# A fused Mamba, attention and expert layer: the first batch's start, reordered

## The chip, the cores and the metric

The kernel runs on one core of a Trainium2 chip. The metric is the device time of one execution in microseconds, lower is better; the number given for a kernel is the median of its runs. The engines are named as the profile names them: PE multiplies matrices, DVE is VectorE, ACT is ScalarE, POOL is GpSimd, and SP issues all transfers of this kernel.

## The reference

One decoder layer over x of 32 batches, 256 tokens, 256 channels, in three blocks, each followed by a layer norm of x plus the block:

```
# 1. state space block, per batch
xc, res = split(x @ W_in.T + b_in)              # 512 channels each
u = silu(causal_conv3(xc) + conv_b)
dlt, Bm, Cm = split(u @ W_x.T)                  # 64, 16, 16
delta = softplus(dlt @ W_dt.T + b_dt)           # the step sizes
carry[t] = exp(delta * A) * carry[t-1] + delta * u * Bm   # 512 x 16 states,
y[t] = sum_n carry[t, :, n] * Cm[t, n]          # restarted every 64 tokens
x = layernorm(x + (y * silu(res)) @ W_out.T + b_out)
# 2. cross attention to ctx (256 tokens), 16 heads of 16
x = layernorm(x + attention(x, ctx))
# 3. experts: token block e of 32 goes through expert e of 8 (256 -> 704 -> 256)
x = layernorm(x + (silu(x @ w1[e]) * (x @ w3[e])) @ w2[e])
```

## The kernel before

All 32 batches go through one pipeline. A batch passes these stages, each a Python generator (a chain) that yields before its next piece of work:

- `pre(b)`: x is transposed on PE (L334) and copied to xT by ACT (L368). PE multiplies it by w_in (`ps_in`, L343). ACT scales the three taps of the convolution into `u` and `shifted` (L390), POOL adds them (L403), ACT evicts `sres` (L349) and applies Silu to `u` (L417) and `sres` (L420) between two table loads (L417, L359).
- `sizes(b)`: the step sizes. PE computes `ps_x` from u and w_x (L434), ACT evicts it as `xp` (L439), PE computes `ps_dt` from xp and w_dt, whose 65th row is b_dt (L343). Softplus is Abs and Relu of ps_dt on ACT (L462, L463), Exp of the first (L466), then on POOL for each of four column blocks a correction `lost` of three operations (L471 to L473), Ln on ACT (L475), and two POOL operations over all four blocks: `delta` (L477) and delta times u, written to `u` (L484). SP stores delta and u to `dd` in DRAM, each when it is ready, and loads C broadcast over partitions (`c_bc`).
- `scan()`: 16 steps a batch. Each loads a strip of dd broadcast over partitions (`ld`, two transfers), ACT computes `da`, the exponentials (`decays`, L561), VectorE the product `bu` (L583, with `b_bc` from PE, L531) and the recurrence `h` (L601). POOL multiplies h by c_bc (`weighted`, L616). After every four steps PE sums over the states into `y` (L630, `sums`), and VectorE multiplies it by sres (L646).
- `mixes`, `keys`, `queries`, `maxima`, `attns`, `finishes`: the projection `ps_out` and the first layer norm, then attention. `maxima` finds the row maxima of the scores (`tops`, L798). The first piece of `mixes` multiplies b_v, spread by VectorE (`bv`, L707), with w_o (`ps_bv`, L711).
- `units`: 32 expert units (L1057, L1119, L1137, L1148), each of one expert over two groups of four batches or of two experts over one group, whose weights come from `fetches` (w13 in transfers of 352 KB, w2 in three). A unit can begin when its batches are stored after attention. Where the first set of buffers is concerned, fetches begin at 50 us of the planner's clock.

The order on every engine is fixed when the kernel is built. `in_order` keeps a clock for each engine from estimated costs (`MM`, `EV`, `VE`, `GP`, and `ISSUE` for a transfer), asks each chain when its next piece can start, and takes the earliest, with a chain's `lag` as the tie breaker; a wait that a chain can't yet answer is `None`. So a chain that starts at another time shifts the order of all that comes later.

Each engine executes its queue in order, SP too: a transfer stands behind those issued before it. Ahead of all chains, the kernel issues the loads of x of batch 0 and of all weights by `dma`. Eight semaphores are used in turn for SP's transfers, so the issue of a transfer waits for the landing of the eighth before it.

Of the kernel before, what the change touches and what calls it, by code (L numbers as in the profile page):

```python
# [10 lines left out]
ALU = mybir.AluOpType  # L11
# [4 lines left out]
P = 128  # L16
B, L, D = 32, 256, 256
DI, NS, DTR = 512, 16, 64
NDC = DI // P
# [78 lines left out]
def decoder_kernel(ctx: ExitStack, tc: tile.TileContext, a: dict, out: bass.AP):  # L98
    nc = tc.nc
    clock = Clock()  # L100
    spend = clock.spend

    def dma(dst, src):

        nc.sync.dma_start(dst, src)  # L105
        spend("SP", ISSUE)
# [82 lines left out]

    w_dt = wp.tile([DTR + 1, DI], F32, name="w_dt")  # L190
    dma(w_dt[:DTR], a["w_dt"])
    for c in range(NDC):
        src = a["b_dt"][:, c : c + 1].rearrange("p o -> o p")
        dma(w_dt[DTR:, c * P : (c + 1) * P], src)
    one = wp.tile([P, 1], F32, name="one")
    nc.gpsimd.memset(one, 0.0)
    nc.gpsimd.memset(one[DTR : DTR + 1], 1.0)
# [4 lines left out]
    for j in range(NJ):  # L202
        for g in range(GB):
            at = a_all[:, j, g].rearrange("p k n -> p (k n)")
            dma(at, src[j, g].unsqueeze(1).to_broadcast([DL, NL, NDC * NS]))
    nc.scalar.preload_act_table_set("natural_log_exp_and_others")
    load_ctx(0)
    w_k, b_k = heads("k")
    w_v = weight("w_v", D, D)
# [4 lines left out]
    b_o = row("b_o")  # L214
    b_v = wp.tile([P, 2, 1], F32, name="b_v")
    dma(b_v, a["b_v"].rearrange("(k p o) -> p k o", p=P, o=1))

# [81 lines left out]

    MM = 0.47
    EV = {1: 0.47, 2: 0.6, 4: 1.06}
    VE = {1: 0.41, 2: 0.69}
    GP = {1: 0.7, 2: 1.27, 4: 2.36}

    def layernorm(tiles, t):
# [49 lines left out]
    def exps():  # L357

        nc.scalar.preload_act_table_set("natural_log_exp_and_others")  # L359
        spend("ACT", 1.28)  # L360

    def pre(b):

# [63 lines left out]
    def sizes(b):  # L427

        yield lambda: us[b][1] if b in us else None, "PE"
        u, t = us[b]  # L430
        yield from take(1, 3, t)
        ps = bank("ps_x")[:, :L]
        for k in range(NDC):
            nc.tensor.matmul(  # L434
                ps[:XP], w_x[:, k, :], u[:, k, :], start=(k == 0), stop=(k == NDC - 1)
            )
        yield spend("PE", NDC * MM), "ACT"
        xp = unit2.tile([P, L], F32, tag="xp", name=f"xp_{b}")
        nc.scalar.activation(xp[:XP], ps[:XP], AF.Identity, bias=one[:XP])  # L439
        t = spend("ACT", EV[1])  # L440
        done(1, t)
        xps[b] = xp
        bcds[b] = bcd.tile([NS, L], F32, tag="bcd", name=f"bcd_{b}")
        yield t, "SP"
        dma(bcds[b], xp[XP - NS : XP])
        yield from take(2, 3, t)
        pss = []
        for c2 in range(2):
            pss.append(
                product(  # L450
                    "ps_dt",
                    lambda j: [w_dt[:, (2 * c2 + j) * P : (2 * c2 + j + 1) * P]],
                    lambda j: [xp[: DTR + 1]],
                )
            )

        yield pss[0][1], "ACT"
        z = unit1.tile([P, NDC, L], F32, tag="delta", name=f"delta_{b}")
        e = unit1.tile([P, NDC, L], F32, tag="e", name=f"ez_{b}")
        for c2, (ps, t) in enumerate(pss):  # L460
            cc = slice(2 * c2, 2 * c2 + 2)
            nc.scalar.activation(e[:, cc], ps, AF.Abs)  # L462
            nc.scalar.activation(z[:, cc], ps, AF.Relu)  # L463
            t = spend("ACT", 2 * EV[2], t)
            done(1, t)
        nc.scalar.activation(e, e, AF.Exp, scale=-1.0)  # L466
        yield spend("ACT", EV[4]), "POOL"
        for c in range(NDC):

            lost = unit1.tile([P, L], F32, tag="lost", name=f"lost_{b}")  # L470
            nc.gpsimd.tensor_scalar(lost, e[:, c], 1.0, -1.0, op0=ALU.add, op1=ALU.add)  # L471
            nc.gpsimd.tensor_tensor(lost, e[:, c], lost, ALU.subtract)  # L472
            nc.gpsimd.tensor_tensor(z[:, c], z[:, c], lost, ALU.add)  # L473
            yield spend("POOL", 3 * GP[1]), "POOL" if c < NDC - 1 else "ACT"
        nc.scalar.activation(e, e, AF.Ln, bias=1.0)  # L475
        yield spend("ACT", EV[4]), "POOL"
        nc.gpsimd.tensor_tensor(z, z, e, ALU.add)  # L477
        yield spend("POOL", GP[4]), "POOL"
        while b >= 2 and b - 2 not in gated:
            yield lambda: gated.get(b - 2), "SP"  # L480
        dds[b] = bcd.tile([2, DI, L], F32, tag="dd", name=f"dd_{b}")
        dma(dds[b][0].rearrange("(c p) t -> p c t", p=P), z)
        load_c(b)
        nc.gpsimd.tensor_tensor(u, z, u, ALU.mult)  # L484
        t = spend("POOL", GP[4])
        yield t, "SP"
        dma(dds[b][1].rearrange("(c p) t -> p c t", p=P), u)
        spread[b] = t + 3.0
        del us[b]
# [4 lines left out]

    def pres():
        for b in range(B):
            yield lambda: 0.0 if len(us) < 2 else None, "PE"
            yield from pre(b)
        while silus:
            silus.pop(0)()  # L500
# [169 lines left out]

    def keys():

        for b in range(B):
            if b:
                load_ctx(b)
            t0 = clock.at["SP"] + LANDING
            ctxT = cts.pop(b)
            yield from take(1, 4, t0)
            ps, t = product(
                "ps_qk",  # L680
                lambda j: [w_k[:, k, j * P : (j + 1) * P] for k in range(2)],
                lambda j: [ctxT[:, k, :] for k in range(2)],
            )
            yield t, "ACT"
            flat = unit1.tile([P, 2, L], F32, tag="k_flat", name=f"k_flat_{b}")
            tk = biased(flat, AF.Identity, b_k, ps, 0)
            done(1, tk)
            yield tk, "SP"
            yield from spread_heads(b, kT, flat, kts)
            yield lambda: max(t0, attended[-1] if b else 0.0) if len(attended) >= b else None, "PE"  # L690
            yield from take(1, 2, t0)
            ps, t = product(
                "ps_v",
                lambda t: [ctxT[:, k, t * P : (t + 1) * P] for k in range(2)],
                lambda t: [w_v[:, k, :] for k in range(2)],
            )
            yield t, "ACT"
            nc.scalar.copy(v[:, :, :, :DK], ps.rearrange("p t (h d) -> p t h d", d=DK))
            vts[b] = spend("ACT", EV[2])
            done(1, vts[b])  # L700

    def mixes():


        yield lambda: spread.get(0), "DVE"
        bv = unit1.tile([P, 2, P], F32, tag="x1T", name="bv")
        nc.vector.tensor_copy(bv, b_v.to_broadcast([P, 2, P]))  # L707
        yield from take(1, 2, spend("DVE", 0.3))
        ps = bank("ps_bv")
        for k in range(2):  # L710
            nc.tensor.matmul(ps[:, :D], bv[:, k, :], w_o[:, k, :], start=(k == 0), stop=(k == 1))  # L711
        yield spend("PE", 2 * MM), "DVE"
        nc.vector.tensor_tensor(b_o, ps[:, :D], b_o, ALU.add)
        done(1, spend("DVE", VE[1]))
        for b in range(B):
            if b >= 2:
                yield lambda: stored[b - 2] + 3.0 if len(stored) >= b - 1 else None, "SP"
            load_x1(b)
            yield clock.at["SP"] + LANDING, "POOL"
            x1 = x1s[b]  # L720
            nc.gpsimd.tensor_tensor(
                x1, x1, b_out.unsqueeze(1).to_broadcast([P, 2, D]), ALU.add
            )
            spend("POOL", GP[2])
            yield lambda: gated.get(b), "PE"
            yield from take(1, 2, gated[b])
            yg = ygs.pop(b)
            ps, t = product(
                "ps_out",
                lambda t: [yg[:, k, t * P : (t + 1) * P] for k in range(NDC)],  # L730
                lambda t: [w_out[:, k, :] for k in range(NDC)],
            )
            yield t, "DVE"
            nc.vector.tensor_tensor(x1, ps, x1, ALU.add)
            t = spend("DVE", VE[2])
            done(1, t)
            t = yield from layernorm([x1[:, t, :] for t in range(2)], t)
            yield lambda: None if x1Ts else t, "PE"
            yield from take(1, 2, t)
            ps, t = transposes(x1)  # L740
            yield t, "ACT"
            x1T = unit1.tile([P, 2, L], F32, tag="x1T", name=f"x1T_{b}")
            nc.scalar.copy(x1T, ps)
            t = spend("ACT", EV[2])
            done(1, t)
            x1Ts[b] = x1T, t
            yield t, "POOL"
            nc.gpsimd.tensor_tensor(x1, x1, b_o.unsqueeze(1).to_broadcast([P, 2, D]), ALU.add)
            spend("POOL", GP[2])
# [406 lines left out]
    def units(bufs):  # L1156
# [9 lines left out]

    xs_at[0] = 10.0
    chains = [
        Chain(decays(), -3.0),
        Chain(weighted(), -2.0),  # L1170
        Chain(scan(), 0.0),
# [79 lines left out]
```

## Time and profile before

| | |
|---|---|
| median of 3 runs | 2941.95 us (2936.0 to 3024.58) |
| the profiled execution | 2947.31 us, its span 2945.6 us |
| PE busy | 2539.0 us (86%) |
| VectorE busy | 2386.1 us (81%) |
| ACT busy | 2041.6 us (69%) |
| POOL busy | 2035.6 us (69%) |
| TensorE clock granted, mean | 0.935 |
| first recurrence (h L601) starts | 71.55 us |
| last recurrence starts | 2631.8 us |

The span is from the first to the last instruction. A line of the timeline gives the start and the length of an instruction in us, its engine and line, what it writes and reads, and in brackets the idle time of its engine before it with what ended that. In a group of the page the two numbers ahead of the second bar are the busy time in us and the mean length in ns; behind it stands the idle time before the group. A matmul of the program in float32 appears as two in the trace (x8 for four).

### The profile page before, as it was taken

The page shows a single profiled execution, that of the slowest core. Times are in us where ns is not written, and L with a number is a line of the kernel's source. Part 1 is how long each engine was busy: PE and PEld are TensorE (multiplying, and loading weights), DVE is VectorE, ACT ScalarE, POOL GpSimd, SP SyncE. Part 2 cuts the span into 40 slices and gives each one's busy share as a digit, 9 for nine tenths or more (in the row PEclk, how much of TensorE's full clock was granted, in tenths as well). Part 3 has the DMA queues.
Part 4 walks back from the last instruction along what each step waited for, and adds up shares of the span by engine and source line. Part 5 has one row for each costly group of instructions (what it writes and reads, how often), then busy time and mean ns, then how long its engine had stood idle before and what let it go on. Part 6 is the DMA issues. An engine that isn't in the chain of part 4 may idle for free. (4 is left out here: it accounts for less than half of the span.)

```text
span 2945.6 us, 48912 instructions
## 1 busy us (share of the span) xinstructions
PE 2539.0 (86%) x16964; PEld 1745.6 (59%) x16964; DVE 2386.1 (81%) x2412; ACT 2041.6 (69%) x4375; POOL 2035.6 (69%) x1562
## 2 busy tenths in 40 slices
PE   6578788888889889988999899889899889789998
PEld 5245455555556556666666566666566556556776
DVE  1899999999999799896999896999988977981222
ACT  5767777877787778776877767787867766654411
POOL 5997987888786787856878856887778756741000
PEclk8689999999999999999999899999999999999999
DMA  5555555555566575564656555566555655654375
GB/s 151 167 165 153 159 161 153 165 150 164 166 176 174 152 200 170 174 181 140 184 170 188 166 159 142 174 181 182 172 165 171 168 154 150 183 167 131 121 233 163
DMA packets 350759, 489.08 MB, mean 166 GB/s; under 512 B 44657, under 2 KB 198513, under 8 KB 350513
## 3 DMA queue, kind: packets, MB, share of 16 engines
q1 hardware_dynamic: 350512, 485.97, 56.9%
q8 instruction: 134, 2.20, 0.3%
q14 instruction: 113, 0.92, 0.1%
HBM read 417.68 MB, written 68.16 MB: 165 GB/s over the span
## 5 line engine op out<-in xcount | busy, mean ns | idle before, releaser
L616 POOL TENSOR_TENSOR h<-h,c_bc 128x1024 f32<-128x1024 f32 x512 | 1206.2, 2361 | 450.0 <-DVE h L601 383.7
L601 DVE TENSOR_TENSOR_SCAN h<-da,bu 128x1024 f32<-128x1024 f32 x512 | 1169.2, 2284 | 57.9 <-PE y L630 11.4
L561 ACT ACTIVATE da<-ld,a_neg 128x252 f32<-128x252 f32 x2048 | 864.0, 500 | 275.0 <-DVE h L601 222.6
L583 DVE TENSOR_TENSOR bu<-ld,b_bc 128x1024 f32<-128x1024 f32 x512 | 626.3, 1223 | 20.4 <-PE b_bc L531 9.1
L630 PE MATMUL y<-h,sel_y 128*32 128x256 f32 x4096 | 338.2, 432 | 136.9 <-POOL h L616 97.0
L776 PE MATMUL s<-qT,kT 64*128 64x256 f32 x2048 | 344.7, 417 | 64.0 <-DMA qT<-tops 23.0
L776 PE MATMUL s<-kT,qT 63*128 63x256 f32 x2048 | 344.2, 416 | 57.1 <-DMA qT<-heads 16.4
L798 DVE TENSOR_REDUCE tops<-s 128x2 f32<-128x512 f32 x512 | 325.1, 677 | 82.3 <-PE s L776 81.6
L853 ACT ACTIVATE es<-s 128x512 f32<-128x512 f32 x512 | 275.8, 593 | 138.4 <-PE s L776 71.9
L630 PEld LDWEIGHTS y<-h,sel_y 128*32 128x32 f32 x4096 | 148.0, 120 | 300.1 <-POOL h L616 147.6
L776 PEld LDWEIGHTS s<-qT,kT 64*128 64x128 f32 x2048 | 215.9, 194 | 169.4 <-issue 45.6
L776 PEld LDWEIGHTS s<-kT,qT 63*128 63x128 f32 x2048 | 220.9, 196 | 158.4 <-issue 48.6
L1057 PE MATMUL ps_h<-x2T,w 128*128 128x256 f32 (+3 forms) x1344 | 304.1, 370 | 10.5 <-ACT x2T L1045 3.9
L343 PE MATMUL ps_in<-xT,w_in 128*128 128x256 f32 x1024 | 261.0, 401 | 15.8 <-ACT xT L368 5.0
L1057 PEld LDWEIGHTS ps_h<-x2T,w 128*128 128x128 f32 (+1 forms) x1344 | 216.5, 184 | 80.1 <-issue 31.7
L343 PEld LDWEIGHTS ps_in<-xT,w_in 128*128 128x128 f32 x1024 | 195.9, 199 | 66.5 <-issue 14.4
L317 POOL TENSOR_SCALAR ln_rstd<-ln_mv 128x2 f32<-128x2 f32 x96 | 21.8, 227 | 291.7 <-DVE ln_mv L314 285.5
L403 POOL TENSOR_TENSOR u<-u,shifted 128x512 f32<-128x512 f32 x128 | 150.9, 1179 | 25.0 <-ACT u L390 20.0
L471 POOL TENSOR_SCALAR lost<-ez 128x256 f32<-128x256 f32 x128 | 137.5, 1074 | 40.9 <-ACT ez L466 39.0
L1137 PE MATMUL ps_down<-w,h 128*128 128x256 f32 (+1 forms) x600 | 152.1, 398 | 5.4 <-DMA w<-in_w 1.9
L823 PE MATMUL ps_oT<-es,v 128*32 128x256 f32 x2048 | 151.2, 406 | 5.1 <-DVE tops L798 4.0
L390 ACT ACTIVATE shifted<-ps_in,tap_b,conv_w 128x256 f32<-128x256 f32 x256 | 130.5, 562 | 26.9 <-PE ps_in L343 20.4
(128 smaller groups left out, 3388.9 us busy)
## 6 DMA issues: line engine op xcount, KB each, us to landing
ld<-dd SPq DMA_DIRECT2D x1024, 256.0 KB
w<-in_w SPq DMA_DIRECT2D x112, 352.0 KB
w13y<-in_w SPq DMA_DIRECT2D x48, 352.0 KB
x<-in_x SPq DMA_DIRECT2D x64, 256.0 KB
dd<-delta SPq DMA_DIRECT2D x32, 512.0 KB
dd<-u SPq DMA_DIRECT2D x32, 512.0 KB
w<-in_w SPq DMA_DIRECT2D x28, 384.0 KB
ctxT<-in_ctxT SPq DMA_DIRECT2D x32, 256.0 KB
```

Of the source, the lines that this page charges most:

```text
L343: nc.tensor.matmul(ps[:, j, :], l, r, start=(k == 0), stop=(k == len(terms) - 1))
L561: nc.scalar.activation(da[:, g, q].rearrange("p (k t) -> p k t", t=CHUNK)[:, :, 1:], loads[i][:, 0, g].rearrange("p (k t) -> p k t", t=CHU ...
L583: nc.vector.tensor_tensor(bu, loads[i][:, 1].unsqueeze(2).to_broadcast([P, GB, NQ, L]), b_bc.unsqueeze(1).to_broadcast([P, GB, NQ, L]), AL ...
L601: nc.vector.tensor_tensor_scan(h.rearrange("p g q t -> p (g q t)"), das_of.pop(i).rearrange("p g q t -> p (g q t)"), bu.rearrange("p g q t ...
L616: nc.gpsimd.tensor_tensor(hs[i], hs[i], c_bc, ALU.mult)
L630: nc.tensor.matmul(y[32 * j : 32 * j + 32, :], sel_y[:, g, :], hs[i - NJ + 1 + j][:, g, q, :], start=(g == 0 and q == 0), stop=(g == GB - ...
L776: nc.tensor.matmul(s[:, t, :], left[r : r + n, g, t * P : (t + 1) * P], right[r : r + n, g, :], start=True, stop=True,)
L798: nc.vector.tensor_reduce(top[:, h % 2, h // 2, :], s, AX.X, ALU.max)
L823: nc.tensor.matmul(oT[32 * j : 32 * j + 32, :], v[:, k, 4 * g + j, :], ess[j][:, k, :], start=(k == 0), stop=(k == 1), tile_position=(0, 3 ...
L853: nc.scalar.activation(es, s, AF.Exp, scale=1.0 / DK**0.5)
L1057: nc.tensor.matmul(ps[:m, i, :], w_tiles[u, which, e][k][:, f * P : f * P + m], right, start=(k == 0), stop=(k == 1),)
L1137: nc.tensor.matmul(po[:, j, :], h[i // m_in][:m, i % m_in, cols], w_tiles[u, "w2", e][f // 3][:m, f % 3, :], start=(i == terms[0]), stop=( ...
```

## The change

Five edits, all about how the first batch begins:

1. b_dt is loaded as one transfer of 512 numbers rather than four of 128.
2. The loads from ctx of batch 0 on (w_k, w_v, b_out, w_out, w_q, w_o and their biases) are no longer issued at once. They are put in a list, `later`, and a new chain, `rest`, issues them one by one in the planner's order; a lag of 50 lets all other chains go first.
3. For batch 0 the operations of the step sizes that POOL did (`lost`, delta, delta times u) are issued on VectorE; the other batches keep POOL.
4. `pres` begins batch 1 only after the step sizes of batch 0 are stored by the planner's clock (`spread[0]`).
5. `keys` and `mixes` begin only after `spread[0]` and once the list is empty.

```diff
     dma(w_dt[:DTR], a["w_dt"])
-    for c in range(NDC):
-        src = a["b_dt"][:, c : c + 1].rearrange("p o -> o p")
-        dma(w_dt[DTR:, c * P : (c + 1) * P], src)
+    dma(w_dt[DTR:], a["b_dt"].rearrange("p c -> c p"))
...
+    later = []
+    now, dma = dma, lambda dst, src: later.append((dst, src))
     load_ctx(0)
     w_k, b_k = heads("k")
...
     dma(b_v, a["b_v"].rearrange("(k p o) -> p k o", p=P, o=1))
+    dma = now
...
-    VE = {1: 0.41, 2: 0.69}
+    VE = {1: 0.41, 2: 0.69, 4: 1.23}
...
+    def rest():
+        while later:
+            yield 0.0, "SP"
+            dma(*later.pop(0))
...
-        yield spend("ACT", EV[4]), "POOL"
+        eng, key, us_ = (nc.gpsimd, "POOL", GP) if b else (nc.vector, "DVE", VE)
+        yield spend("ACT", EV[4]), key
         for c in range(NDC):
             lost = unit1.tile([P, L], F32, tag="lost", name=f"lost_{b}")
-            nc.gpsimd.tensor_scalar(lost, e[:, c], 1.0, -1.0, op0=ALU.add, op1=ALU.add)
-            nc.gpsimd.tensor_tensor(lost, e[:, c], lost, ALU.subtract)
-            nc.gpsimd.tensor_tensor(z[:, c], z[:, c], lost, ALU.add)
+            eng.tensor_scalar(lost, e[:, c], 1.0, -1.0, op0=ALU.add, op1=ALU.add)
+            eng.tensor_tensor(lost, e[:, c], lost, ALU.subtract)
+            eng.tensor_tensor(z[:, c], z[:, c], lost, ALU.add)
...
-        nc.gpsimd.tensor_tensor(z, z, e, ALU.add)
+        eng.tensor_tensor(z, z, e, ALU.add)
...
-        nc.gpsimd.tensor_tensor(u, z, u, ALU.mult)
-        t = spend("POOL", GP[4])
+        eng.tensor_tensor(u, z, u, ALU.mult)
+        t = spend(key, us_[4])
...
     def pres():
         for b in range(B):
+            if b == 1:
+                yield lambda: spread.get(0), "PE"
             yield lambda: 0.0 if len(us) < 2 else None, "PE"
...
     def keys():
+        yield lambda: None if later else spread.get(0), "SP"
...
     def mixes():
-        yield lambda: spread.get(0), "DVE"
+        yield lambda: None if later else spread.get(0), "DVE"
...
     chains = [
+        Chain(rest(), 50.0),
```

In the instruction order that results, the list is still issued before batch 0's step sizes are stored; the load of batch 1's x now stands within it, ps_dt of batch 0 stands directly behind its ps_x on PE, and the first expert weights stand between the store of batch 0's delta times u and the first load of a strip.

More of the change, by code (lines that the diff above doesn't have):

```diff
@@ L466, in sizes @@
         nc.scalar.activation(e, e, AF.Exp, scale=-1.0)
-        yield spend("ACT", EV[4]), "POOL"
+        eng, key, us_ = (nc.gpsimd, "POOL", GP) if b else (nc.vector, "DVE", VE)
+        yield spend("ACT", EV[4]), key
         for c in range(NDC):
             lost = unit1.tile([P, L], F32, tag="lost", name=f"lost_{b}")
-            nc.gpsimd.tensor_scalar(lost, e[:, c], 1.0, -1.0, op0=ALU.add, op1=ALU.add)
-            nc.gpsimd.tensor_tensor(lost, e[:, c], lost, ALU.subtract)
-            nc.gpsimd.tensor_tensor(z[:, c], z[:, c], lost, ALU.add)
-            yield spend("POOL", 3 * GP[1]), "POOL" if c < NDC - 1 else "ACT"
+            eng.tensor_scalar(lost, e[:, c], 1.0, -1.0, op0=ALU.add, op1=ALU.add)
+            eng.tensor_tensor(lost, e[:, c], lost, ALU.subtract)
+            eng.tensor_tensor(z[:, c], z[:, c], lost, ALU.add)
+            yield spend(key, 3 * us_[1]), key if c < NDC - 1 else "ACT"
         nc.scalar.activation(e, e, AF.Ln, bias=1.0)
-        yield spend("ACT", EV[4]), "POOL"
-        nc.gpsimd.tensor_tensor(z, z, e, ALU.add)
-        yield spend("POOL", GP[4]), "POOL"
+        yield spend("ACT", EV[4]), key
+        eng.tensor_tensor(z, z, e, ALU.add)
+        yield spend(key, us_[4]), key
         while b >= 2 and b - 2 not in gated:
```

## The prediction

> **What bounds the kernel now.** I read three views: the timeline of the first 75 us, the groups of the page, and a count of each engine's queue between fixed points of the scan.
>
> The timeline (start, length, engine, line, idle before it and what ended the idle) shows that the loop proper opens at 70 us:
>
> ```profile
> 26.04 0.48 ACT L439 ACTIVATE xp<-ps_x,one 97x256 f32<-97x256 f32 x1 [1.09 <-PE ps_x L434]
> ...
> 30.44 0.39 SPq L105 DMA_DIRECT2D x<-in_x  x1
> ...
> 33.85 1.12 PE L334 MATMUL ps_tr<-ident,x 128*128 128x128 f32 x4 [7.85 <-DMA x<-in_x]
> ...
> 34.76 3.62 PE L343 MATMUL ps_dt<-xp,w_dt 65*128 65x256 f32 x8
> ...
> 40.53 1.09 POOL L471 TENSOR_SCALAR lost<-ez 128x256 f32<-128x256 f32 x1 [19.42 <-ACT ez L466]
> ...
> 61.02 2.34 POOL L484 TENSOR_TENSOR u<-delta,u 128x1024 f32<-128x1024 f32 x1
> ...
> 70.17 1.23 DVE L583 TENSOR_TENSOR bu<-ld,b_bc 128x1024 f32<-128x1024 f32 x1 [1.84 <-DMA ld<-dd]
> 71.55 2.29 DVE L601 TENSOR_TENSOR_SCAN h<-da,bu 128x1024 f32<-128x1024 f32 x1
> ```
>
> Two delays stand in it. xp is ready at 26.52, but ps_dt starts at 34.76: on PE it is queued behind the transposes of batch 1's x, which left SP only at 30.44, after all weights. Then POOL needs from 40.53 to 63.36 to finish the step sizes, sharing itself with batch 1's L403 additions. VectorE does 5.5 us of work in all of 0 to 70.2.
>
> Afterwards the scan sets the pace:
>
> ```profile
> L616 POOL TENSOR_TENSOR h<-h,c_bc 128x1024 f32<-128x1024 f32 x512 | 1206.2, 2361 | 450.0 <-DVE h L601 383.7
> L601 DVE TENSOR_TENSOR_SCAN h<-da,bu 128x1024 f32<-128x1024 f32 x512 | 1169.2, 2284 | 57.9 <-PE y L630 11.4
> ```
>
> 512 scans run from 71.55 to 2634.1, 5.0 us each, with VectorE busy about 90%. PE-bound expert units fill the remaining 311 us. So an earlier first scan is worth its microseconds at the end, unless the loop gives them back.
>
> **Part 1: b_dt in one DMA.** The four b_dt issues took 3.81 us, of which 1.4 are a wait for w_in. One issue (0.59 by its neighbours), after the same wait, saves some 1.7 us of SP. The word after it, a_log, is not late (a_neg waits for ACT till 24.69), and the 512 pieces of 4 bytes are the same: nothing.
>
> **Part 2: ps_dt right after ps_x.** The instruction order of the changed kernel is known before it runs; on PE its four ps_dt products precede the transposes of batch 1's x. They start at 26.57 (0.05 after xp, as at 60.04 to 60.09) rather than 34.76: 8.2 us. Their length depends on the clock:
>
> ```profile
> 24.00:26.00 2.00, 2.00 (x6) 1.01 (x4) 0.20 (x1) 0.94 (x2) 0.00 (x0) 0.59 1.17 281
> 26.00:28.00 2.00, 0.00 (x0) 0.00 (x0) 0.00 (x0) 0.48 (x1) 0.00 (x0) 1.00 0.92 85
> 34.00:36.00 2.00, 2.00 (x7) 1.77 (x8) 0.00 (x0) 0.59 (x1) 0.00 (x0) 0.50 0.00 0
> ```
>
> (The third number from the right is the granted clock.) The ps_dt row, 3.62 us at clock 0.50, would put Exp's end at 26.57 + 5.69 = 32.3. [...] ps_x has just been busy for 3.51 us, and the trace grants 1.00 at 26 to 28, to an idle PE. [...]
>
> **Part 3: step sizes on VectorE.** Twelve 128x256 operations and two of 128x1024. Nearest rows: L646, 0.42; L583, 1.23, both with PSUM operands. No row shows this TENSOR_SCALAR on VectorE; L548's 0.20 at 64 columns bounds it below, 0.6 above. At 0.45 each: 30.7 + 5.4 = 36.1; Ln (1.06) to 37.2; delta to 38.5; u to **39.8**. VectorE and POOL were idle there, so the work costs nothing elsewhere. Ends: 38.8 and 41.6. POOL loses 14.8 us.
>
> **Part 4: what is late next.** Not the load. SP has after dd<-u: four w13 loads, an x, three w2 loads and batch 0's x1, nine issues (0.57 each), before ld: issued at 45.9. By the row (second ld of step 0 issued 65.96, bu at 70.17) it lands 4.2 us after the second issue, 50.7. [...] It is hidden by ACT.
>
> ACT takes batch 1's xT only after Ln, at 37.2, and its queue then holds batch 1's whole preparation before the first da. PE is cold again: first product 37.85 to 41.5. The nearest row for the rest is batch 0's own preparation, undisturbed: first L390 at 10.82, table load ended at 24.68, 13.86 us. So 41.5 + 13.86 = 55.4; da of step 0 takes 1.65; first scan **57.1**, against 71.55: **14.5 us** earlier (12.9 with the cold clock). The new wait of PE (ps_bv for bv, on VectorE behind u) has bv at 40.2 and PE there at about 44; behind it stand sres's products and b_bc, due by 49. Nothing, with 4 us of cover. If ld came after 55.4, each us would cost one.
>
> Batches 0 and 1: POOL's queue from first to 32nd h holds 65.5 + 64.2 us after, 60.3 + 63.5 before (rows of h, lost, L403), since batch 1's step sizes are now made inside the loop; the loop took 64.1 and 65.7 there with POOL 95% busy. Part of the difference shows: **+2.5**, up to +6.
>
> **Part 5: the loop is planned anew.** The changed start changes every later decision of the planner. I cut PE's queue at each 64 sel_y matmuls (one batch) and priced it by rows per matmul (s 0.34, ps_in 0.51, ps_h 0.45, y 0.165, ps_oT 0.15). Before, six of batches 2 to 31 hold over 84 us; they sum to 578.6 and took 576.1, so they are PE-bound; the other 24 took 77.4 each whatever they held. After, eight hold over 84 and sum to 727.0. So 22 x 77.4 + 724 = 2427, before 2433: **-6**. At the last scan 19 expert units are done in both queues, so the last 311 us stand.
>
> **Sum.** Profiled execution 2947.3 - 14.5 + 2.5 - 6 = **2929**. The median of the runs is 5.4 below that execution, so it could come out near 2924; I keep 2929.
>
> **Rivals.**
> - *Head start eaten at the borders (0.13).* Batch 1's and 2's step sizes are stored only after the load of step 15 of the batch before, where before they were 4 and 6 steps ahead. For it: POOL's full queue. Against: by my chain POOL finishes u at 113, one load from the need. If both borders stall 5 us: 2929 + 10 = 2939.
> - *Crammed batches cost more than their PE sum: slower (0.25).* In before's batch 28, 93.8 us were taken for 87.4. At that 1.073 the eight cost 780 rather than 724: 2929 + 56 = 2985. It outweighs the gain from a rate of about 1.03. For it: the eight batches between 13 and 27 lie close together. Against: the mean of six was 0.996.
> - *The change doesn't do what it says (0.07).* ld really waits behind the weights until 65 or so and the first scan moves by 5 us: 2938.
>
> **How the numbers follow.** Main forecast 0.55: 2929. A straight-line fit of before's batch lengths on those PE sums misses a batch by about 3.5 us; over thirty batches that is 19 us in either kernel and 26 in the difference of two. That gives 2895 to 2965, and leaves out the slow rival's upper half and a lucky loop. 2% is 59 us, about what a measurement of this kernel can tell from no change: faster by that 0.03, within 0.93, slower 0.04.
>
> **What would show it.** Right: ps_dt near 26.6 at clock 1.00; u on VectorE near 40; first scan at 56 to 59, released by ACT's da; scan 16 near 122. Wrong: first scan released by ld; VectorE and ACT waiting for ld at the first step of batches 1 and 2; a last scan not near 2616, with the excess in batches 13 to 27.

## The result

| | before | after |
|---|---|---|
| median, 4 runs each | 2944.92 us | 2977.78 us |
| the profiled execution | 2947.31 us | 2968.68 us |
| its span | 2945.6 us | 2966.9 us |
| first scan starts | 71.5 | 58.8 |
| scan 0 to scan 32 (batches 0 and 1) | 129.9 | 138.9 |
| scan 32 to the last, 511 (the loop) | 2430.4 | 2440.8 |
| last scan to the end (the tail) | 313.8 | 328.4 |

(Scans are counted from 0, 16 to a batch. All rows below the median are of the one profiled execution, in us.)

The changed kernel takes **1.0111** of the time before, 95% interval [1.0068, 1.0155]: slower by about 1%, where 2929 us and a small gain were forecast. (One run of each kernel was disturbed, 4588.83 us after and 3024.58 before; the ratio leaves both out.)

The profiled execution of after was the quickest of its four runs, so the two profiles lie 21.3 us apart and the medians 33. The sum that follows is that of the profiles: -12.7 to the first scan, +9.1 in batches 0 and 1, +10.4 in the loop, +14.6 behind it, together +21.4. The head start is real. Most of it is given back within two batches (at scan 32 the changed kernel is still 3.7 us ahead), and then 10.4 and 14.6 us are lost.

Three groups of the page of after:

```profile
L628 POOL TENSOR_TENSOR h<-h,c_bc 128x1024 f32<-128x1024 f32 x512 | 1206.2, 2361 | 434.4 <-DVE h L613 382.7
L613 DVE TENSOR_TENSOR_SCAN h<-da,bu 128x1024 f32<-128x1024 f32 x512 | 1169.1, 2283 | 72.5 <-PE y L642 24.8
...
L595 DVE TENSOR_TENSOR bu<-ld,b_bc 128x1024 f32<-128x1024 f32 x512 | 626.4, 1223 | 25.2 <-DMA ld<-dd 12.2
```

None of the three became dearer (their means before: 2361, 2284 and 1223 ns). What grew is idle time, above all that ahead of the scan, 57.9 to 72.5 us, and its share that waits for PE's y, 11.4 to 24.8.

The timeline of after, in the head (start, length, engine, line, tiles, idle before it and what ended that):

```profile
22.30 3.73 PE L442 MATMUL ps_x<-u,w_x 128*97 128x256 f32 x8 [6.32 <-ACT u L425]
...
26.07 0.47 ACT L447 ACTIVATE xp<-ps_x,one 97x256 f32<-97x256 f32 x1 [1.30 <-PE ps_x L442]
...
26.59 3.78 PE L345 MATMUL ps_dt<-xp,w_dt 65*128 65x256 f32 x8 [0.56 <-ACT xp L447]
...
32.47 0.30 DVE L481 TENSOR_SCALAR lost<-ez 128x256 f32<-128x256 f32 x1 [7.48 <-ACT ez L474]
...
37.06 1.06 ACT L485 ACTIVATE ez<-ez 128x1024 f32<-128x1024 f32 x1 [4.62 <-DVE lost L482]
...
39.51 1.23 DVE L494 TENSOR_TENSOR u<-delta,u 128x1024 f32<-128x1024 f32 x1
...
42.28 1.02 ACT L398 ACTIVATE shifted<-ps_in,tap_b,conv_w 128x256 f32<-128x256 f32 x2 [3.69 <-PE ps_in L345]
...
56.46 1.69 ACT L573 ACTIVATE da<-ld,a_neg 128x252 f32<-128x252 f32 x4 [0.34 <-DMA ld<-dd]
...
57.49 1.23 DVE L595 TENSOR_TENSOR bu<-ld,b_bc 128x1024 f32<-128x1024 f32 x1 [12.19 <-DMA ld<-dd]
58.82 2.29 DVE L613 TENSOR_TENSOR_SCAN h<-da,bu 128x1024 f32<-128x1024 f32 x1
```

Its order is as forecast: ps_dt at 26.6, step sizes on VectorE ready at 40.7, first scan at 58.8. Note the ACT rows: 4.62 us idle for VectorE, then 3.69 for PE. ACT had nothing else in its queue there, since batch 1's xT stands behind Ln. The same timeline at the border of batches 0 and 1:

```profile
78.14 1.10 POOL L481 TENSOR_SCALAR lost<-ez 128x256 f32<-128x256 f32 x1
...
102.89 6.96 POOL L628 TENSOR_TENSOR h<-h,c_bc 128x1024 f32<-128x1024 f32 x3
...
109.82 2.35 POOL L487 TENSOR_TENSOR delta<-delta,ez 128x1024 f32<-128x1024 f32 x1
...
111.25 0.42 DVE L658 TENSOR_TENSOR yg<-y,sres 128x256 f32<-128x256 f32 x1 [5.39 <-PE y L642]
...
112.19 0.36 SPq L105 DMA_DIRECT2D dd<-delta  x1
...
125.78 4.51 ACT L573 ACTIVATE da<-ld,a_neg 128x252 f32<-128x252 f32 x11
...
127.63 2.29 DVE L613 TENSOR_TENSOR_SCAN h<-da,bu 128x1024 f32<-128x1024 f32 x1 [3.71 <-ACT da L573]
...
154.81 0.42 DVE L658 TENSOR_TENSOR yg<-y,sres 128x256 f32<-128x256 f32 x1 [3.40 <-PE y L642]
```

VectorE stands 5.39 us for a y whose last h POOL finished at 109.85, after a queue without a gap. Batch 1's delta leaves at 112.19, 15 us before batch 1's first scan (before, it left at 99.49, 36 us ahead). That scan waits another 3.71 us for ACT, which had pieces of the next batches' preparation in front: batch 2's softplus and batch 3's convolution (116.48 to 125.8; a piece of it waited for the store of batch 1's u at 114.62). From scan 12 (103.6 us, against 120.5 before) to scan 16 the lead shrinks from 16.9 us to 8.1. In before, the timeline lists one wait of VectorE between scan 0 and scan 32:

```profile
96.60 0.42 DVE L646 TENSOR_TENSOR yg<-y,sres 128x256 f32<-128x256 f32 x1 [4.44 <-PE y L630]
```

In after the waits of that stretch sum to 14.1 us (the three shown, one of 0.55 and one of 1.08). The difference, 9.7, is about the 9.1 us by which batches 0 and 1 are longer.

### The profile page after: what moved, and what is told of

Same layout as the page of the kernel before. It is cut to its first block, busy times and chain, and to the rows that moved or that the text cites. A ratio compares the mean times of both kernels' runs of the same rounds, so it can differ in the third digit from the quotient of the medians.

```text
span 2966.9 us, 48885 instructions
## 1 busy us (share of the span) xinstructions
PE 2538.8 (86%) x16964; PEld 1746.9 (59%) x16964; DVE 2393.3 (81%) x2426; ACT 2040.8 (69%) x4367; POOL 2020.6 (68%) x1548
## 4 chain that ended last, share of the span: by engine, by line
PE 33%; DVE 26%; POOL 15%; ACT 9%; issue 9%; DMA 7%; SPq 1%; DVEq 0%; ACTq 0%; POOLq 0%
DVE h L613 13%; POOL h L628 7%; PE ps_h L1070 7%; DVE bu L595 7%; PE s L789 6%; PE y L642 4%; PE ps_down L1150 4%; DVE tops L811 4%; ACT da L573 4%; PE ps_in L345 3%; DMA ld<-dd 2%; POOL lost L481 2%; PE ps_oT L836 2%; DMA w<-in_w 1%; POOL lost L482 1%
## 5 line engine op out<-in xcount | busy, mean ns | idle before, releaser
L628 POOL TENSOR_TENSOR h<-h,c_bc 128x1024 f32<-128x1024 f32 x512 | 1206.2, 2361 | 434.4 <-DVE h L613 382.7
L613 DVE TENSOR_TENSOR_SCAN h<-da,bu 128x1024 f32<-128x1024 f32 x512 | 1169.1, 2283 | 72.5 <-PE y L642 24.8
L595 DVE TENSOR_TENSOR bu<-ld,b_bc 128x1024 f32<-128x1024 f32 x512 | 626.4, 1223 | 25.2 <-DMA ld<-dd 12.2
L789 PE MATMUL s<-qT,kT 64*128 64x256 f32 x2048 | 336.7, 412 | 57.2 <-DVE tops L811 15.9
L789 PE MATMUL s<-kT,qT 63*128 63x256 f32 x2048 | 338.1, 412 | 49.9 <-DVE tops L811 14.7
```

The source lines that it names most:

```text
L595: nc.vector.tensor_tensor(bu, loads[i][:, 1].unsqueeze(2).to_broadcast([P, GB, NQ, L]), b_bc.unsqueeze(1).to_broadcast([P, GB, NQ, L]), AL ...
L613: nc.vector.tensor_tensor_scan(h.rearrange("p g q t -> p (g q t)"), das_of.pop(i).rearrange("p g q t -> p (g q t)"), bu.rearrange("p g q t ...
L628: nc.gpsimd.tensor_tensor(hs[i], hs[i], c_bc, ALU.mult)
L789: nc.tensor.matmul(s[:, t, :], left[r : r + n, g, t * P : (t + 1) * P], right[r : r + n, g, :], start=True, stop=True,)
```

## The experiments

A span is split here as in the table above: first scan; batches 0 and 1; loop; tail. The parts are those of one profile a run; the ratios are those of the runs' times against the kernel before in the same session.

**1. Only the head, in the old order.** The order that the planner had made for the kernel before is written down as a string of chains and replayed. Batch 0's step sizes are moved ahead in it, their fourteen operations put on VectorE, and b_dt comes in one transfer. All else keeps its place.

```diff
-    while True:
-        live = [(c, c.time()) for c in chains if not c.over]
...
+    for c in zlib.decompress(base64.b85decode(ORDER)).decode():
+        chains[ord(c) - 97].step(clock, 0.0)
...
+        eng = nc.gpsimd if b else nc.vector
```

> The head of the change alone: b_dt in one transfer, batch 0's step sizes finished on VectorE and stored before batch 1's preparation is begun on PE, ACT and POOL, and every queue otherwise in the order of the kernel before, written down and replayed instead of planned. Theory 'order' (the head is worth some microseconds, and the loss comes from the new order of loop and tail): ACT still has batch 1's step sizes and part of batch 2 ahead of the first da, so the first scan starts near 66 (before 71.5), scan 32 is 4 to 5 us early, that is kept to the last scan and the tail stays 314 us: ratio 0.998, 4 to 5 us faster. Theory 'head' (starting early is itself what costs: POOL's debt and the collisions of loads come back later): the last scan is not early, or late, ratio 1.00 to 1.01.

Measured: 2939.11 us, ratio 0.9983 [0.9972, 0.9993], within what the theory 'order' said. First scan 68.8 (66 had been expected), batches 0 and 1 129.4, scan 32 at 198.2. The first scan comes only 2.7 us earlier, since ACT still works through batch 1's preparation first. But what is gained is still there at scan 32 (3.2 us) and in the median (5.3). So the step sizes on VectorE are not what makes after slower. (The profile is that of the quickest of twenty runs: its loop took 2418.1 where that of before, in the same order, took 2430.4.)

**2. Batch 0's step sizes back on POOL, in the changed order.**

```diff
-        eng, key, us_ = (nc.gpsimd, "POOL", GP) if b else (nc.vector, "DVE", VE)
+        eng = nc.gpsimd
+        key, us_ = ("POOL", GP) if b else ("DVE", VE)
```

> The changed kernel's order on every queue but one move: batch 0's fourteen operations go back to POOL, at the same places of the plan, VectorE loses them. Theory 'order': u of batch 0 is ready some 7 us later (12 operations at 0.85 on average instead of 0.39, two at 2.36 instead of 1.23), the first scan 7 us later than in the changed kernel, and batches 2 to 31 and the tail keep their excess of 25 us over the kernel before: about 2974 to 2980 in the profiled execution, ratio to before 1.01 to 1.015. Theory 'POOL': the early batches are bound by POOL in the loop, not by the first scan, and POOL is idle before it: scan 32 starts within 2 us of the changed kernel's.

Measured: 2982.84 us, 1.0143 [1.0115, 1.0171] of before. First scan 63.5, 4.7 later than in after; scan 32 at 202.5, 4.8 later; last scan 6.3 later. Seven us had been expected at the first scan; 1.8 of them are missing because ps_dt ran at the full clock in this profile (1.99 us, 3.78 in after). A delay at the head arrives whole at scan 32 as long as the order stays. The reading that POOL's load in batches 0 and 1 swallows it falls.

**3. How much is the draw of the order?** The booked cost of a recurrence, which only the planner reads, is changed in the kernel before and in the changed kernel. Nothing but the order moves.

```diff
-            recurred[i] = spend("DVE", 2.29)
+            recurred[i] = spend("DVE", 2.31)
```

(2.28 and 2.34 in the others. The first three runs are of the kernel before, the last three of the changed one.)

> The kernel before with one number of the planner changed, the cost it books for a recurrence (2.31 for 2.29); no instruction is added or taken away, only the order of the loop moves. Theory 'order': the time moves by 10 to 30 us either way, as crammed batches (PE work over 84 us) fall elsewhere. Theory 'head': the order doesn't matter at this scale, within 5 us of the kernel before.

> The kernel before, planned cost of a recurrence 2.28 for 2.29. Theory 'lottery' (the order of the loop is a draw; the changed kernel drew badly): between 2915 and 2970, no nearer to the kernel before than 2.31 was (2922). Theory 'penalty' (the change's held-back chains make every plan worse by some 25 us): the same spread here, and all plans of the changed kernel stand above all plans of this one.

> The kernel before, planned cost of a recurrence 2.34. As p_b28: 2915 to 2970.

> The changed kernel with the same number of the planner changed (2.31 for 2.29). Theory 'order': the first scan stays at 58 to 59, and the end moves by 10 to 30 us either way, it may well come out below the kernel before. Theory 'head': stays 20 to 35 us above the kernel before, as the changed kernel is.

> The changed kernel, planned cost of a recurrence 2.28. Lottery: 2915 to 2970, a mean over the plans of the changed kernel that lies 0 to 5 us below the mean of before's plans. Penalty: 2950 to 2990, and the mean of four plans 20 us or more above that of before's four.

> The changed kernel, planned cost of a recurrence 2.34. As p_a28. First scan at 58 to 59 in both.

| booked | head | median us | ratio to before | first scan | batches 0, 1 | loop | tail |
|---|---|---|---|---|---|---|---|
| 2.31 | before | 2922.23 | 0.9939 [0.9918, 0.9961] | 71.4 | 130.7 | 2386.8 | 330.0 |
| 2.28 | before | 2964.83 | 1.0060 [1.0041, 1.0079] | 70.9 | 132.2 | 2408.7 | 352.1 |
| 2.34 | before | 2974.84 | 1.0097 [1.0072, 1.0121] | 71.0 | 136.6 | 2420.0 | 345.2 |
| 2.31 | changed | 2963.88 | 1.0074 [1.0048, 1.0100] | 57.5 | 138.7 | 2427.9 | 330.7 |
| 2.28 | changed | 2943.96 | 0.9996 [0.9984, 1.0007] | 58.3 | 139.2 | 2395.2 | 346.9 |
| 2.34 | changed | 2968.33 | 1.0075 [1.0053, 1.0097] | 59.1 | 139.8 | 2423.6 | 343.5 |

Two things follow. The order alone is worth from -22 to +29 us: the plans of the kernel before spread over 53 us, more than the effect in dispute. With the two originals the means of four are 2951.6 and 2963.5; their difference is 12, with a standard error of 14. That is neither what 'lottery' said (0 to 5 us below) nor what 'penalty' said (20 or more above, and every changed plan above every plan of before, which 2943.96 refutes; 2974.84 also lies above the range that was given), so the loop and the tail of after may be no more than a poor draw. Batches 0 and 1 look like more than a draw: they take 138.7 to 139.8 in every plan with the changed head and 129.9 to 136.6 without it.

**4. Is it POOL's load in batch 1?** Batch 1's fourteen operations go to VectorE too, in the changed order.

```diff
-        eng, key, us_ = (nc.gpsimd, "POOL", GP) if b else (nc.vector, "DVE", VE)
+        eng = nc.vector if b < 2 else nc.gpsimd
+        key, us_ = ("POOL", GP) if b else ("DVE", VE)
```

> The changed kernel's order on every queue, but batch 1's fourteen step size operations too are issued on VectorE, at the same places of the plan; POOL loses 14.8 us of work inside batch 0's scan and VectorE gains some 7. Theory 'POOL debt' (batches 0 and 1 took 68.8 and 70.1 us, 9 us longer than before, because POOL makes batch 1's step sizes between the products h): scan 32 starts 5 to 9 us earlier than in the changed kernel (near 190 in place of 197.8), and the end moves by the same. Theory 'ACT and SP' (the first da of batch 1 is late because ACT has batch 2's preparation ahead of it, and SP's loads stand behind the store of delta): scan 32 stays within 3 us of 197.8, and VectorE's 7 us more come on top.

Measured: 2977.69 us, 1.0123 [1.0107, 1.0140]; batches 0 and 1 took 145.2, six more than in after. From 58.8 to 127.6 us POOL is busy 37.0 us rather than 56.6, and the delta is stored later still, at 117.84. The theory 'POOL debt' missed, in sign: scan 32 comes at 203.4, 5.6 later. (The other said within 3 us of 197.8 and also 7 us more on VectorE, which can be read either way.) The timeline of this run tells why:

```profile
79.00 2.49 DVE L483 TENSOR_TENSOR lost<-ez,lost 128x256 f32<-128x256 f32 x1
...
100.67 2.35 POOL L629 TENSOR_TENSOR h<-h,c_bc 128x1024 f32<-128x1024 f32 x1 [1.33 <-DVE h L614]
100.75 2.56 DVE L483 TENSOR_TENSOR lost<-ez,lost 128x256 f32<-128x256 f32 x1
...
109.94 0.42 DVE L483 TENSOR_TENSOR lost<-ez,lost 128x256 f32<-128x256 f32 x1
```

The same operation took 0.42 us beside an idle POOL and 2.5 while POOL multiplied an h. Five of the twelve `lost` operations were stretched so, by 8 us together, and batch 0 took 6.6 us longer. So this run took a load off POOL and put a stretched one on VectorE: it doesn't tell what POOL's load alone costs. The place of batch 1's step sizes was still to be tried.

**5. The fourth edit taken back.** Batch 1's preparation no longer waits for batch 0's step sizes; all other edits stand, and the planner plans for itself.

```diff
         for b in range(B):
-            if b == 1:
-                yield lambda: spread.get(0), "PE"
             yield lambda: 0.0 if len(us) < 2 else None, "PE"
```

> The changed kernel without its fourth edit: batch 1's preparation no longer waits for batch 0's step sizes, all else stands. In the queues batch 1's delta is now stored after the load of step 10 of batch 0, as before the change, and not after that of step 15. Theory (the fourth edit pushes batch 1's preparation and step sizes into the loop, and this is what batches 0 and 1 pay for): from the first to the 32nd scan 129 to 132 us (129.8 before, 129.4 in the first experiment) rather than 138.9, with no idle of VectorE of over 3 us at the border of batches 0 and 1; the first scan comes later than 58.8, between 60 and 67, since ACT has two preparations before it; scan 32 by 198. Rival (what batches 0 and 1 pay comes of something else in the changed order, such as the expert weights and the list of loads in front of the first strip): still 138 to 140 us, as in all four plans of the changed kernel. Everything after scan 32 is planned anew, so the time as a whole may lie anywhere in 2940 to 2985 and tells nothing of either.

Measured: **2927.53 us, 0.9951 [0.9935, 0.9966]** of before. Batches 0 and 1 took 131.5 and no idle of over 3 us is left at the border (one wait for y, 3.99 us at 80.9, stands in the middle of batch 0, as one of 4.44 does in before); the theory holds. It was wrong on two counts, both on the fast side: the first scan comes at 56.3, before that of after, and the time lies below the 2940 to 2985 that were given. The timeline of this run:

```profile
26.07 1.89 PE L345 MATMUL ps_in<-xT,w_in 128*128 128x256 f32 x8
...
27.80 1.89 PE L345 MATMUL ps_dt<-xp,w_dt 65*128 65x256 f32 x8
...
36.56 2.49 POOL L411 TENSOR_TENSOR u<-u,shifted 128x512 f32<-128x512 f32 x2 [3.19 <-ACT u L398]
36.60 1.42 DVE L482 TENSOR_TENSOR lost<-ez,lost 128x256 f32<-128x256 f32 x1
...
45.01 1.23 DVE L494 TENSOR_TENSOR u<-delta,u 128x1024 f32<-128x1024 f32 x1
...
51.24 1.09 POOL L481 TENSOR_SCALAR lost<-ez 128x256 f32<-128x256 f32 x1 [12.20 <-ACT ez L474]
...
54.39 1.23 DVE L593 TENSOR_TENSOR bu<-ld,b_bc 128x1024 f32<-128x1024 f32 x1 [0.44 <-PE b_bc L541]
54.60 3.68 ACT L571 ACTIVATE da<-ld,a_neg 128x252 f32<-128x252 f32 x9
...
56.34 2.29 DVE L611 TENSOR_TENSOR_SCAN h<-da,bu 128x1024 f32<-128x1024 f32 x1 [0.72 <-ACT da L571]
...
83.93 0.54 SPq L105 DMA_DIRECT2D dd<-delta  x1
```

Batch 0's u is finished 5.5 us later than in after (46.2 against 40.7), yet everything after it is earlier: batch 1's preparation has been done meanwhile. Its lost starts on POOL at 51.24 rather than 78.14, and its delta leaves at 83.93 rather than 112.19. The windows of the two runs (stretch, length, then busy time and count of PE, weight loads, VectorE, ACT and POOL, granted clock, DMA share, GB/s), first after, then this run:

```profile
26.00:42.00 16.00, 8.02 (x21) 6.14 (x21) 7.23 (x15) 5.12 (x8) 0.00 (x0) 0.50 0.27 64
...
58.80:127.60 68.80, 43.01 (x203) 26.58 (x201) 57.05 (x35) 53.53 (x117) 56.60 (x36) 0.77 0.62 172
```

```profile
56.30:119.90 63.60, 34.95 (x181) 21.23 (x180) 57.14 (x35) 49.80 (x112) 59.53 (x39) 0.74 0.69 189
...
26.00:42.00 16.00, 10.95 (x49) 9.18 (x49) 6.42 (x12) 14.43 (x26) 4.78 (x4) 0.93 0.67 187
```

From 26 to 42 us ACT works 5.12 us in after and 14.43 here. That is the time in which the softplus of batch 0 goes back and forth between PE, ACT and VectorE; the fourth edit leaves it empty, and its work has to be done later, between the scans. In batch 0 POOL is busier here (59.53) than in after (56.60), and the batch is 5.2 us shorter. Once more it isn't the amount of work but its place.

There is more in this run. Laid beside before's trace, its queues are the same on all five engines from the end of batch 0 on: the last row that differs starts at 97 us on PE (a few matmul records missing from a trace aside), 106 on ACT, 110 on SP and 116 on POOL, and on VectorE nothing but the fourteen new operations differs. Accordingly its loop takes 2427.8 and its tail 311.6, beside 2430.4 and 313.8. In the changed kernel's queue on PE some 700 of 1709 rows differ from before. So it is the fourth edit that made the planner take another order. The span of after exceeds that of this run by 39.7 us: 2.5 at the first scan, 7.4 in batches 0 and 1, 13.0 in the loop and 16.8 in the tail. The first two are what the edit costs up to scan 32 (a part of the 2.5 is the clock of ps_dt: the changed plan booked at 2.31, where ps_dt ran at the full clock as here, began at 57.5), the last two the order that came with it.

**6. The tail in the old order.** The changed kernel's order is replayed up to the last scan, and the steps left then are done in the sequence in which the kernel before did them. (The loop of `in_order` is again replaced by a string; a step that isn't possible yet is kept back.)

```diff
+    behind = []
+    for c in zlib.decompress(base64.b85decode(ORDER)).decode():
+        behind.append(chains[ord(c) - 97])
...
+            if behind[k].time() is None or behind[k] in behind[:k]:
+                k += 1
+            else:
+                behind.pop(k).step(clock, 0.0)
```

> The changed kernel's order replayed as it is up to the last scan, and from there the steps that are left in the order in which the kernel before did them (a step that the planner can't yet do waits for the next place; five steps of expert units and four fetches more are left than before, and 29 steps of attention and eight others fewer). Theory (the order planned for the tail makes it 14.6 us longer): from the last scan to the end about 314 us, 309 to 319, the time about 2962. Rival (the state at the last scan makes it: one transfer of w13 more and five steps of units more are left, and weights come late in any order): 326 to 332 us, the time within 5 us of 2977.

Measured: 3013.59 us, 1.0237 [1.0214, 1.0259], the tail 368.4. Neither theory said so. The run shows that the order of the tail alone is worth 40 us, and not why after's is 14.6 longer. It gives one more number: up to the last scan its queues are those of after, and its loop took 2448.9 in the profile where after's took 2440.8. So two executions of one order can differ by eight us in the loop (by twelve in before's order, experiment 1), where the sum above has 10.4.

The profiles of all runs together say more than a single one. Four have after's order in the loop and three before's:

| order | runs | loop | tail |
|---|---|---|---|
| before's | before, experiments 1 and 5 | 2430.4, 2418.1, 2427.8 | 313.8, 312.2, 311.6 |
| after's | after, experiments 2, 4 and 6 | 2440.8, 2442.3, 2448.2, 2448.9 | 328.4, 330.5, 327.2 (6: another tail) |

They don't overlap. On average after's order costs 20 us in the loop and 16 in the tail. With -12.7 and +9.1 ahead of them that makes 32, which is what the medians say (33); the profile of after, its quickest run, shows too little.

**7. A better version.** The head of experiment 1 with the written-down order of the plan booked at 2.31.

> The head of e_head with the written down order of p_b31 in place of that of the kernel before. Theory 'order': the head's gain is the same 4 to 5 us whatever order follows, so some 2917 against p_b31's 2922, ratio to before 0.991 to 0.993. If the gain doesn't add up (loop bound elsewhere in that order): 2922 or above.

Measured: 2912.48 us, 0.9908 [0.9887, 0.9929]; it beats both kernels, and what was expected (0.991 to 0.993) by a hair. Most of it is the order (0.9939 alone).

## Why the prediction was wrong

Its sum was -14.5 + 2.5 - 6 + 0 = -18; the profiles show -12.7 + 9.1 + 10.4 + 14.6 = +21.4. Of the 39.4 us between them, 1.8 lie in the head, 6.6 in batches 0 and 1, 16.4 in the loop and 14.6 in the tail.

**The step that failed** is Part 5. It priced the new order of the loop by PE's work alone, as a gain of 6 us, and put the tail at nothing because the same number of units was done; after's order costs 20 us in the loop and 16 in the tail (seven profiles, table above). Part 4's +2.5 for batches 0 and 1 failed with it, at +9.1. Both go back to the fourth edit, to which the prediction gave no price of its own: without it (experiment 5) batches 0 and 1 take 131.5, loop and tail are those of before, and the kernel is 0.5% faster. Two of the signs of being wrong that the prediction had named came true: the first scan waited for ld, and the last scan came at 2638.5, with the excess in batches 13 to 27.

- **ps_dt right after ps_x: place right, clock wrong.** Forecast 26.57, measured 26.59. The granted clock stayed at 0.50 and the products took 3.78 us instead of 1.9, so Exp ended at 32.4, near the 32.3 of the prediction's row at clock 0.50. The sum starts from an end of Exp at 30.7, with ps_dt at clock 1.00 and 1.9 us; that the clock would be full behind ps_x was the author's estimate, and no run shows that it must be. The row of before with 1.00 granted at 26 to 28 showed only how the clock's changes fell in that one execution. With this head, ps_x of 3.73 us and then ps_dt after 0.56 us of idle, ps_dt ran at clock 0.50 (3.78 us) in seven profiles and at 1.00 (1.99 us) in two (in one of them, experiment 2, Exp ended at 30.8). It cost some 1.7 us. The traces tell when: in before and in after the changes of the granted clock all lie a whole multiple of 3.41 us apart (115 and 133 stretches between them, the shortest of 3.41 us), and this grid lies differently in each. The clock went to 1.00 behind ps_x in before, in experiments 2 and 5 and in the changed plan booked at 2.31; there the 3.41 us ahead of the change held 3.12 to 3.35 us of ps_x. In after no stretch of the grid held more than 2.57, and it stayed at 0.50. So that the clock came up in before was luck.
- **Step sizes on VectorE: right.** TENSOR_SCALAR took 0.29 to 0.30 (0.45 was estimated, 0.20 to 0.6 the bounds), TENSOR_TENSOR 0.42, the wide ones 1.23; twelve operations 5.0 us against 5.4. POOL was idle beside them (from 20.9 to 45.2 us), and none took longer; beside a working POOL five took 1.22 to 2.56 us in experiment 4, and two took 1.42 and 1.28 in experiment 5.
- **ld or ACT: ACT's time right, ld's too early.** ACT's table load ended at 56.11, which is 42.28 + 13.83 (13.86 was taken from batch 0's own row). ld was issued at 48.82, three us later than reckoned, and bu had it at 57.49, where the nearest row had given 50.7. The cover that ACT was to give (its table load was reckoned to end at 55.4) was gone: da waited 0.34 for ld, and the first scan began 0.1 us after the bu that had waited for ld. It came about 1 us later than ACT alone would have had it (56.11 + 1.69 = 57.8). The forecast of 57.1 missed 58.8 by these two, the clock and ld.
- **Batches 0 and 1: the term that failed first.** +2.5, up to +6, was forecast and +9.1 measured. The step priced POOL's load (65.5 against 60.3 in batch 0). But experiment 5 left POOL busier in batch 0 than after (59.5 us against 56.6) and the batch was shorter. The step should have priced the place: the store of batch 1's delta had moved from after step 10's load to after step 15's, and ACT's idle time in the head was a free place for batch 1's preparation. The rival "head start eaten at the borders" had the mechanism, late step sizes, and about the size (10 us). The waits came as 5.39 us within batch 0, 3.71 at its border and 3.40 within batch 1.
- **The loop: -6 forecast, +10.4 measured.** The cut of PE's queue found the eight heavy batches (13, 15, 16, 19, 20, 23, 25, 27) and their 727.0 us; they took 747.3, or 1.028 of it, where 0.996 was estimated. The 22 light ones took 77.1 against 77.4. The slow rival said 1.073 and a turning point near 1.03, so it named the right place at about a third of its size. As a rule it doesn't hold: over all runs with other orders the heavy batches took 0.988 to 1.009 of their sums, and only this order took 1.022 to 1.028, in four profiles. What in it costs the 20 us of these batches is not settled.
- **The tail: 0 forecast, +14.6 measured.** "At the last scan 19 expert units are done in both queues, so the last 311 us stand" took the count for the time. With 19 units done the tail took 311.6 to 313.8 in the old order (three profiles), 327 to 331 in the changed order (three) and in the changed kernel's plan booked at 2.31; with 17 or 18 it took 330 to 352. PE's work in the tail hardly differs (290.2 after, 288.0 before), its idle time does, 38 us against 26. The chain of waits from 2600 us on says what for, after first, then before:

```profile
by line: PE ps_h L1070 32.4%; PE ps_down L1150 18.1%; PE s L789 7.1%; DMA w<-in_w 7.0%; DMA w2y<-in_w 5.5%; DVE h L613 2.5%; issue 2.5%; DVE bu L595 2.2%; PE ps_oT L836 1.7%; DMA xe<-x2d 1.7%; DMA out<-xe 1.7%; DVE tops L811 1.6%; PE ps_qk 
```

```profile
by line: PE ps_h L1057 36.4%; PE ps_down L1137 16.5%; PE s L776 7.1%; DMA w13y<-in_w 5.3%; DVE h L601 3.3%; DMA xe<-x2d 2.3%; DMA w<-in_w 2.3%; DMA w2y<-in_w 2.2%; PE ps_oT L823 2.2%; SPq L105 2.1%; POOL h L616 2.1%; PE ps_out L343 1.5%; is
```

The shares are of 367 and 346 us. Expert weights (the `in_w` entries) stand on the chain with 12.5% of the one, 46 us, and 9.8% of the other, 34; with `w13y` of after, 4.2 us and below the lines that are printed, it is 50 against 34. Over the runs in either order it is 48 to 50 us against 20 to 34. So the tail of after's order waits more for its weights. The prices of PE's work couldn't show that. Why the weights come later in that order no run separates.

Above all, the prediction gave no term to the fact that a new order is a new draw. The range of 26 us for the loop was near the spread that experiment 3 found, but it was centred on the gain. And the fourth edit was costed inside ACT's chain (the 13.86 us behind Ln) and never against its omission. Without it, the gain between the profiles is 18.4 us; that this is the very size of the forecast is luck, since the forecast was for the kernel with the edit and had a gain of 6 in the loop.

**What stays open.** Whether the orders that follow the fourth edit are worse by nature or by chance: four against four, loop and tail take 2759 against 2747 us on average, within the spread. Nor was it settled what makes this order's heavy batches dear, and its weights late in the tail.

## What to carry to other kernels

When a first stage is shortened by holding the second stage back, look at what the engines do while the first one's chain runs back and forth: if they idle, the held-back work has lost its free place and comes back between the steps of the loop, where it costs (here 9.1 of the 12.7 us that were gained). Where a planner fixes the order, any edit is also a new draw; measure a few plans of both kernels before a per cent is put down to the edit, or replay a written-down order. And carry a delay from stage to stage in a table of fixed points (first scan, scan 32, last scan, end), since the sign of each stage can differ.

## What the runs showed of the hardware

- VectorE's `lost` operations with two inputs in SBUF (128x256, float32) took 0.42 us with POOL idle, and 1.28 to 2.56 us while POOL ran an addition of 1.2 us (experiment 5) or a multiplication of 2.35 (experiment 4). The one of 2.56 us began 0.08 us behind the start of an h of 2.35 and ended 0.29 behind its end. The TENSOR_SCALAR, which has one such input, took 0.27 to 0.30 and once, beside an h, 1.22. bu, whose b_bc comes from PSUM, took its 1.22 us beside the same h too. Moving work from POOL to VectorE was cheap where POOL was idle, as at batch 0 in after (twelve operations in 5.0 us), and was not in experiment 4 (8 us more for twelve).
- The full clock is not to be counted on for a product that follows one busy stretch of 3.7 us: behind ps_x, ps_dt had it in two profiles of nine. In before and after the clock changed on a grid of 3.41 us, and in the four profiles named above in which it came up behind ps_x, the 3.41 us ahead of the change held 3.12 us of ps_x or more. In experiment 5 it came up at 25.98, still under ps_x; the products that fill the gap behind it began at 26.07, so they are not the cause. The 3.78 us of ps_dt didn't bring it up: in experiment 1, where ps_dt ran from 26.46 to 30.24, the clock was 0.50 up to 32, and ps_in at 38.51 still took 3.78 us, where at 44.66 it took 1.89.
